# Moving convolution sums behind the softmax terms, and three weight spreadings to the end of their slices, in a fused attention and convolution kernel

## Chip, cores, metric

The kernel runs on one core of a Trainium2 chip. The metric is device microseconds of one execution, median of several runs. PE is TensorE, DVE is VectorE, ACT is ScalarE, POOL is GpSimd, SP is SyncE, which here issues nearly all DMAs.

## What is computed

The input x has 16 images of 56 x 56 pixels and 384 channels. Two layers follow each other, each with a residual and each behind a group normalisation over 32 groups:

```
x = x + attention(group_norm(x))      # layer 0
x = x + depthwise3x3(group_norm(x))   # layer 1, weights sign(clip(w))
```

Attention projects to q, k, v (384 to 1152), splits the channels into 3 groups of 4 heads of 32, and for each pixel takes a softmax over the 9 neighbours of a 3 x 3 window whose dilation is 1, 2 or 3 by group:

```
attn = softmax(einsum('bgdn,bgdkn->bgnk', q, unfold(k)) * 32**-0.5)
out  = einsum('bgnk,bgdkn->bgnd', attn, unfold(v))
y    = out @ w_proj.T + b_proj
```

All data is float32.

## The kernel before

An image is cut into 7 chunks of 8 rows (448 pixels); there are 112 chunks m, and c is the chunk's place in its image. Work is written as pieces that are put on a list of slices with `at(when, order, piece)`. Pieces are emitted by slice, and inside a slice by `order`, a number of the list at the end (SOFTMAX 0, SCORE 1, STATISTICS, CONVOLVE, WEIGH, QUERY, SPREAD, QKV, PROJECT, STAGE_A, STAGE_C, NORM, LOADS). A chunk advances every 9 slices (STEP), so several chunks are in flight. The tile framework's scheduler then makes each engine's instruction order out of what was emitted, and sets semaphores and buffers; it may move an instruction against its neighbours, except where `in_one_go` keeps matmuls together. Every engine runs its own order, SP too.

`plan_a` loads a chunk and transposes it (PE writes `pt_x`, ACT copies to `xa`, DVE takes statistics, SP stores it to `xd`).

`plan_b(m, t0)`, t0 = 9m, is the attention of one chunk:

- `k_or_v` and `query` (L463): PE projects into `pkv` and `pq`; ACT copies `pkv` to the k and v tiles (L473).
- `score(i)`, i = 0 to 8 (slice t0+i): DVE multiplies q with three shifted windows of k into `t` (L516). At i = 2, 5, 8 PE sums over the 32 channels of each head into `ps` (L501, 128x32 column tiles, 8, 8 and 11 matmuls).
- `softmax_1` to `softmax_5` (slices t0+9 to t0+12): ACT copies `ps` to `sT`, PE transposes it into `pt_s`, DVE and ACT make the softmax `ew`. Then `ew` is split into three bf16 terms that add up to it, all in the tile `e`: ACT casts the first (L555), POOL subtracts it (`rest`, L559), casts the second (L563) and subtracts for the third (L564).
- `turn_weights` (L569): SP issues one transposing DMA of `e` into `aT`.
- `weigh(i)`, i = 0 to 8 (slice t0+14+i): three bf16 matmuls spread `aT` over the channels into `pb_a` (L582, row tiles of 24 rows; one PSUM buffer of three banks). DVE multiplies with windows of v into `w` (L589). POOL adds the products (L597) and at every third i adds the three taps into `y` (L600, L601).
- `out_project(j)`: PE multiplies `y` with w_proj into `po` (L615); DVE adds bias and residual into `xr`, takes statistics, and SP stores to `x1d`.

`plan_c(m, t0)`, t0 = 9(m + 10), is the convolution of one chunk, ten chunks later. Channels 0 to 255 are convolved by PE (`convolve`: `pc`, L710, 32-column tiles). Channels 256 to 383 are done without PE: ACT scales nine shifted windows of `zg` into three `m` tiles (`taps_g`, L761), POOL adds these (L767), then the three planes and the residual (`sum_g`, L772, L775) into `xg`. `turn` transposes the result into `pt_o`, ACT copies it to `osb`, SP stores it. Where c = 0 the pieces `normalise_g` and `taps_g` come one slice later (`late`), for they need the statistics of the whole image. The last image (b = 15) takes another way, with DVE.

Seen from plan_c's chunk m, the softmax of chunk m + 9 falls into the slices t0 to t0+3.

Small PSUM results (`pt_x`, `pt_o`, `pt_s`, `pkv`, `po`, `pc`) rotate over three banks (`ps_mt`): each is written when the reader of the third before it has finished.

Of the kernel before, what the change touches and what calls it, by code (L numbers as in the profile page):

```python
# [1 line left out]

# [10 lines left out]
ALU = mybir.AluOpType  # L13
# [10 lines left out]
ROWS = 8  # L24
# [11 lines left out]
def dilated_attention_then_binary_conv(  # L36
# [28 lines left out]
    nc = tc.nc  # L65
# [10 lines left out]
    def place(p):  # L76

        g, o = divmod(p, NTAP)
        return NG * o + g
# [82 lines left out]
    for which, slots in enumerate((K_SLOTS, V_SLOTS)):  # L162
        kv.append([])
        for g, d in enumerate(DIL):
            kv[which].append([])
            for s in range(slots):
                t = const.tile([P, ROWS + 2 * d, W + 2 * d], F32, name=f"{'kv'[which]}_{g}_{s}")
# [11 lines left out]
    for s in range(2):  # L179
        t = const.tile([P, ROWS + 2, W + 2], F32, name=f"zg_{s}")  # L180
# [100 lines left out]
    def rows(ap):  # L281
        return ap.rearrange("p (r w) -> p r w", w=W)

    def three(t, d, ky):

        tw = t[:, ky * d : ky * d + ROWS, 0:W]
        return bass.AP(tw.tensor, tw.offset, [tw.ap[0], (d, 3), *tw.ap[1:]])

    def in_one_go(matmuls):

        matmuls[0]()
        with tc.high_priority():
            for m in matmuls[1:]:
                tc.keep_in_program_order(m())
# [97 lines left out]
    def at(when, order, piece):  # L392

        pieces.setdefault((when, order), []).append(piece)
# [2 lines left out]
    xd, x1d = {}, {}  # L397
    mr0, mr1 = {}, {}
    first = {}

    def plan_a(m, t0):

# [42 lines left out]
    def plan_b(m, t0):  # L445

        b, c = divmod(m, NCH)
        had = {}
# [102 lines left out]
        term = [e3.rearrange("p s u (r k) -> p (s u r) k", r=4)[:, :, 8 * t : 8 * t + 8] for t in range(TERMS)]  # L551
# [9 lines left out]
        def softmax_5():  # L561
            r8 = had["rest"].rearrange(EIGHTS, k=8)
            nc.gpsimd.tensor_copy(term[1], r8)  # L563
            nc.gpsimd.tensor_tensor(term[2], r8, term[1], ALU.subtract)  # L564

        def turn_weights():

# [5 lines left out]
        def weigh(i):  # L573

            g, ky = divmod(i, 3)
            pb = ps_bc.tile([P, 3, 512], F32, tag="bc", name="pb_a")

            def copy(kx):
                v = place(3 * i + kx)
                lo = 32 * (v // 2 % 4)  # L580
                rows_of = slice(lo, lo + 2 * TERMS * HEADS)
                return nc.tensor.matmul(  # L582
                    pb[:, kx, :PX].rearrange("p (s n) -> p s n", s=NSUB), spread[rows_of, v % 2, :],
                    had["a"][rows_of, :, v // 8, :], start=True, stop=True
                )

            in_one_go([lambda kx=kx: copy(kx) for kx in (2, 0, 1)])
            w = w_p.tile([P, 3, PX], F32, tag="w", name="w")
            nc.vector.tensor_tensor(  # L589
                w.rearrange("p k (r w) -> p k r w", w=W),  # L590
                pb[:, :, :PX].rearrange("p k (r w) -> p k r w", w=W), three(kv[1][g][m % V_SLOTS], DIL[g], ky), ALU.mult,
            )
            if ky == 0:
                had["w0"] = w
                return
            w0 = had["w0"]
            nc.gpsimd.tensor_tensor(w0, w0, w, ALU.add)  # L597
            if ky == 2:
                had[f"y{g}"] = y = y_p.tile([P, PX], F32, tag="y", name="y")
                nc.gpsimd.tensor_tensor(y, w0[:, 0], w0[:, 1], ALU.add)  # L600
                nc.gpsimd.tensor_tensor(y, y, w0[:, 2], ALU.add)  # L601
# [34 lines left out]
        at(t0 + 11, SOFTMAX, softmax_3)  # L636
        at(t0 + 11, SOFTMAX, softmax_4)
        at(t0 + 12, SOFTMAX, softmax_5)
        at(t0 + 12, LOADS, turn_weights)
        for i in range(9):  # L640
            at(t0 + 14 + i, WEIGH, lambda i=i: weigh(i))
        at(t0 + 20, LOADS, load_residual)
        for j in range(NG):
            at(t0 + 24 + j, PROJECT, lambda j=j: out_project(j))
# [1 line left out]
    def plan_c(m, t0):  # L646

        b, c = divmod(m, NCH)
        p0 = c * PX
        had = {}  # L650
# [93 lines left out]
        def taps_last(ky):  # L744
# [5 lines left out]
            for kx in range(3):  # L750
# [3 lines left out]
                    acc if o else mid, op0=ALU.mult, op1=ALU.add,  # L754
                )

        def taps_g(ky):
            t = m_p.tile([P, 3, PX], F32, tag="m", name="m")
            for kx in range(3):
                o = 3 * ky + kx  # L760
                nc.scalar.activation(  # L761
                    rows(t[:, kx]), zp[:, ky : ky + ROWS, kx : kx + W], AF.Copy, scale=ktap[:, o : o + 1]
                )
            if ky == 0:
                had["m"] = t
            else:
                nc.gpsimd.tensor_tensor(had["m"], had["m"], t, ALU.add)  # L767

        def sum_g(kx):
            t = had["m"]  # L770
            if kx < 3:
                nc.gpsimd.tensor_tensor(t[:, 0], t[:, 0], t[:, kx], ALU.add)  # L772
            else:
                mid = had["xg"][:, 1 : ROWS + 1, :].rearrange("p r w -> p (r w)")
                nc.gpsimd.tensor_tensor(mid, t[:, 0], mid, ALU.add)  # L775

        def turn(s):
            pt = ps_mt.tile([P, 512], F32, tag="mt", name="pt_o")
# [32 lines left out]
        for ky in range(3):  # L811
            at(t0 + 2 * ky + late, CONVOLVE, lambda ky=ky: taps_g(ky))
        for kx in (1, 2, 3):
            at(t0 + 5 + kx, CONVOLVE, lambda kx=kx: sum_g(kx))
# [5 lines left out]
        for s in range(NSUB):  # L820
            at(t0 + 9 + s, STAGE_C, lambda s=s: turn(s))

    SOFTMAX, SCORE, STATISTICS, CONVOLVE, WEIGH, QUERY, SPREAD, QKV, PROJECT, STAGE_A, STAGE_C, NORM, LOADS = range(13)

    STAT_ORDER = (STATISTICS, SPREAD, SPREAD, SPREAD, STATISTICS, SPREAD)
    STEP = 9
# [45 lines left out]
    for m in range(N):  # L872
        plan_a(m, start_a(m))
        plan_b(m, STEP * m)
        plan_c(m, STEP * (m + 10))
# [31 lines left out]
```

## Time and profile before

| what | us |
|---|---|
| median of 3 runs | 5328.02 (5322.63 to 5328.53) |
| profiled execution | 5318.41 |
| its span | 5316.7 |
| PE busy | 5131.6 (97%) |
| DVE busy | 4206.7 (79%) |
| POOL busy | 4255.0 (80%) |
| ACT busy | 2310.1 (43%) |
| mean granted TensorE clock | 0.981 |

The profile is one execution of the program. A line of the timeline gives the start, the duration, engine, source line, operation, what it writes and reads, and the shape; idle time before it and what ended it stand in brackets. Matmuls overlap, so what one of them costs is the distance from its start to the next start. An fp32 matmul of these leaves two records, so "x6" of `po` are three matmuls. A stage's row gives its length, each engine's busy time with its instructions, then the granted clock (1.00 is full), the share of the DMA engines, and GB/s. In the middle of the run a chunk takes about 44 to 46 us.

### The profile page before, as it was taken

The numbers are of one execution on the slowest core, as the hardware profiler recorded it, in microseconds if no ns is written. First come the engines' busy times: TensorE is split into PE (matmuls) and PEld (weight loads), VectorE is DVE, ScalarE is ACT, GpSimd is POOL, SyncE is SP. The second block draws the span as 40 slices with busy tenths as digits, with TensorE's granted clock in tenths as the row PEclk, the third lists the DMA queues.
The fourth block names the chain that finished last, engine by engine and source line by source line (L and its number), as shares of the span: only waits on it lengthen the run. The fifth ranks groups of instructions, "written<-read, shape, count | busy, mean of one in ns | idle before, by whom it ended". The sixth has DMA issues, their size and how long they took to land. (4 is left out here: it accounts for less than half of the span.)

```text
span 5316.7 us, 75544 instructions
## 1 busy us (share of the span) xinstructions
PE 5131.6 (97%) x26885; PEld 2336.1 (44%) x26885; DVE 4206.7 (79%) x4125; ACT 2310.1 (43%) x4077; POOL 4255.0 (80%) x2950
## 2 busy tenths in 40 slices
PE   8999999999999999999999999999999999999976
PEld 4444444444444444444444444444444444444433
DVE  5887887878878788887888878788887888878764
ACT  3223444444444444444444444444444444444443
POOL 2677888888888888888888888888888888888881
PEclk8999999999999999999999999999999999999987
DMA  6434565556555565666555556555565555554545
GB/s 194 134 105 116 165 164 158 164 156 163 162 158 161 157 164 157 165 161 165 161 159 164 150 161 165 162 161 160 166 165 155 162 149 164 146 137 134 134 133 155
DMA packets 811630, 825.62 MB, mean 155 GB/s; under 512 B 360307, under 2 KB 801014, under 8 KB 811254
## 3 DMA queue, kind: packets, MB, share of 16 engines
q1 hardware_dynamic: 803270, 808.79, 55.5%
q10 hardware_dynamic: 7984, 12.00, 0.7%
q8 instruction: 213, 3.49, 0.3%
q14 instruction: 163, 1.34, 0.1%
HBM read 466.41 MB, written 231.21 MB: 131 GB/s over the span
## 5 line engine op out<-in xcount | busy, mean ns | idle before, releaser
L597 POOL TENSOR_TENSOR w<-w 128x1344 f32<-128x1344 f32 x672 | 2071.5, 3083 | 522.1 <-DVE w L589 500.8
L589 DVE TENSOR_TENSOR w<-pb_a,v 128x1344 f32<-128x1344 f32 x1008 | 1555.3, 1543 | 274.0 <-PE pb_a L582 235.8
L516 DVE TENSOR_TENSOR t<-pq,k 128x1344 f32<-128x1344 f32 x1008 | 1536.8, 1551 | 251.5 <-PE pq L463 251.0
L463 PE MATMUL pkv<-xn,wqkvT 128*128 128x448 f32 x3924 | 1565.9, 548 | 0.4 <-DVE xr L618 0.4
L463 PEld LDWEIGHTS pkv<-xn,wqkvT 128*128 128x128 f32 x3924 | 718.4, 190 | 668.8 <-issue 643.0
L615 PE MATMUL po<-y,wprojT 128*128 128x448 f32 x2016 | 835.2, 551 | 41.8 <-POOL y L601 32.4
L696 ACT ACTIVATE z<-z,mrz 96x448 f32<-96x448 f32 x840 | 578.4, 751 | 662.9 <-DMA z<-x1d 427.6
L463 PE MATMUL pq<-xn,wqkvT 128*128 128x448 f32 x1962 | 856.0, 572 | 0.0
L767 POOL TENSOR_TENSOR m<-m 128x1344 f32<-128x1344 f32 x210 | 640.1, 3048 | 152.9 <-ACT m L761 148.8
L501 PE MATMUL ps<-t,sel 128*32 128x448 f32 x6048 | 659.4, 545 | 7.9 <-DVE t L516 6.9
L761 ACT ACTIVATE m<-zg,ktap 128x448 f32<-128x448 f32 x945 | 555.5, 659 | 8.6 <-POOL xg L775 1.7
L615 PEld LDWEIGHTS po<-y,wprojT 128*128 128x128 f32 x2016 | 376.9, 192 | 400.8 <-issue 336.2
L710 PE MATMUL pc<-z,kdiag 96*32 96x440 f32 (+1 forms) x5040 | 515.5, 542 | 4.8 <-POOL z L698 4.4
L463 PEld LDWEIGHTS pq<-xn,wqkvT 128*128 128x128 f32 x1962 | 352.0, 194 | 327.3 <-issue 327.3
L582 PE MATMUL pb_a<-aT,spread 24*128 24x448 bf16 x3024 | 369.6, 360 | 71.7 <-DMA aT<-e 60.4
L618 DVE SCALAR_TENSOR_TENSOR xr<-po,bias,xr 128x448 f32<-128x448 f32 x336 | 228.5, 680 | 220.0 <-PE po L615 215.1
L601 POOL TENSOR_TENSOR y<-y,w 128x448 f32<-128x448 f32 x336 | 381.6, 1136 | 16.3
L600 POOL TENSOR_TENSOR y<-w 128x448 f32<-128x448 f32 x336 | 381.4, 1135 | 13.6
L473 ACT COPY v<-pkv 128x448 f32<-128x448 f32 x336 | 176.3, 525 | 487.8 <-PE pkv L463 470.0
L717 DVE TENSOR_TENSOR x<-pc,x 128x448 f32<-128x448 f32 x224 | 138.5, 618 | 276.1 <-PE pc L710 275.9
L582 PEld LDWEIGHTS <-spread 24*128 24x128 bf16 x3024 | 98.5, 91 | 560.9 <-issue 481.0
L473 ACT COPY k<-pkv 128x448 f32<-128x448 f32 x336 | 178.8, 532 | 381.0 <-PE pkv L463 381.0
(132 smaller groups left out, 4311.0 us busy)
## 6 DMA issues: line engine op xcount, KB each, us to landing
z<-x1d SPq DMA_DIRECT2D x570, 224.0 KB, 3.9
xr<-xd SPq DMA_DIRECT2D x112, 672.0 KB, 4.2
x1d<-xr SPq DMA_DIRECT2D x112, 672.0 KB, 3.2
xn<-xd SPq DMA_DIRECT2D x109, 672.0 KB, 4.6
xin<-in_x_dram SPq DMA_DIRECT2D x105, 672.0 KB, 7.2
xd<-xa SPq DMA_DIRECT2D x315, 224.0 KB, 3.4
out_dram<-osb SPq DMA_DIRECT2D x420, 168.0 KB, 3.5
x<-x1d SPq DMA_DIRECT2D x112, 448.0 KB, 8.2
```

The costliest lines, as they stand in the source:

```text
L463: nc.tensor.matmul(dst[:, :PX], wqkvT[:, cc, o0 : o0 + P], had["xn"][:, cc, :], start=(cc == 0), stop=(cc == NG - 1))
L501: return nc.tensor.matmul(had["ps"][32 * j : 32 * j + 32, :PX], sel[:, s0 : s0 + 32], tk, start=(issued[j] == 1), stop=(issued[j] == len(r ...
L516: nc.vector.tensor_tensor(t.rearrange("p k (r w) -> p k r w", w=W), q3, k3, ALU.mult)
L582: return nc.tensor.matmul(pb[:, kx, :PX].rearrange("p (s n) -> p s n", s=NSUB), spread[rows_of, v % 2, :], had["a"][rows_of, :, v // 8, :] ...
L589: nc.vector.tensor_tensor(w.rearrange("p k (r w) -> p k r w", w=W), pb[:, :, :PX].rearrange("p k (r w) -> p k r w", w=W), three(kv[1][g][m ...
L597: nc.gpsimd.tensor_tensor(w0, w0, w, ALU.add)
L601: nc.gpsimd.tensor_tensor(y, y, w0[:, 2], ALU.add)
L615: nc.tensor.matmul(po[:, :PX], wprojT[:, g, j * P : (j + 1) * P], had[f"y{g}"], start=(g == 0), stop=(g == NG - 1))
L696: nc.scalar.activation(z, z, AF.Identity, bias=mrz[:, j, q, 0:1], scale=mrz[:, j, q, 1:2])
L710: return nc.tensor.matmul(pcr[q * HD : (q + 1) * HD, :, lo:hi], kdiag[:, kx, j * NQ + q, :], rows(set_of(j, q))[:, :, lo + kx - 1 : hi + k ...
L761: nc.scalar.activation(rows(t[:, kx]), zp[:, ky : ky + ROWS, kx : kx + W], AF.Copy, scale=ktap[:, o : o + 1])
L767: nc.gpsimd.tensor_tensor(had["m"], had["m"], t, ALU.add)
```

## The change

Two things are changed.

The POOL sums of the convolution get an order of their own where c = 0: the last sum of taps (ky = 2) and the three pieces of `sum_g` are told to be issued on POOL behind the last softmax term of chunk m + 9. `tc.issue_after(ins)` adds, to each instruction of its block, an edge for the order on the engine, with no semaphore.

The pieces `weigh(2)`, `weigh(5)` and `weigh(8)` of each chunk get a later place inside their slice, WEIGH_LATE, behind CONVOLVE, PROJECT, STAGE_A and STAGE_C. The next slice begins with the score of i = 8, 2 or 5 of the next chunk, whose `ps` matmuls then follow.

```diff
+    last_term = {}
...
         def softmax_5():
             r8 = had["rest"].rearrange(EIGHTS, k=8)
             nc.gpsimd.tensor_copy(term[1], r8)
-            nc.gpsimd.tensor_tensor(term[2], r8, term[1], ALU.subtract)
+            last_term[m] = nc.gpsimd.tensor_tensor(term[2], r8, term[1], ALU.subtract)
...
         for i in range(9):
-            at(t0 + 14 + i, WEIGH, lambda i=i: weigh(i))
+            at(t0 + 14 + i, WEIGH_LATE if i % 3 == 2 else WEIGH, lambda i=i: weigh(i))
...
+        def behind_softmax(wanted):
+            if c or not wanted:
+                return nullcontext()
+            return tc.issue_after(last_term[m + 9].ins)
+
         def taps_g(ky):
...
             if ky == 0:
                 had["m"] = t
             else:
-                nc.gpsimd.tensor_tensor(had["m"], had["m"], t, ALU.add)
+                with behind_softmax(ky == 2):
+                    nc.gpsimd.tensor_tensor(had["m"], had["m"], t, ALU.add)
 
         def sum_g(kx):
             t = had["m"]
-            if kx < 3:
-                nc.gpsimd.tensor_tensor(t[:, 0], t[:, 0], t[:, kx], ALU.add)
-            else:
-                mid = had["xg"][:, 1 : ROWS + 1, :].rearrange("p r w -> p (r w)")
-                nc.gpsimd.tensor_tensor(mid, t[:, 0], mid, ALU.add)
+            with behind_softmax(True):
+                if kx < 3:
+                    nc.gpsimd.tensor_tensor(t[:, 0], t[:, 0], t[:, kx], ALU.add)
+                else:
+                    mid = had["xg"][:, 1 : ROWS + 1, :].rearrange("p r w -> p (r w)")
+                    nc.gpsimd.tensor_tensor(mid, t[:, 0], mid, ALU.add)
...
-    SOFTMAX, SCORE, STATISTICS, CONVOLVE, WEIGH, QUERY, SPREAD, QKV, PROJECT, STAGE_A, STAGE_C, NORM, LOADS = range(13)
+    SOFTMAX, SCORE, STATISTICS, CONVOLVE, WEIGH, QUERY, SPREAD, QKV, PROJECT, STAGE_A, STAGE_C, WEIGH_LATE, NORM, LOADS = range(14)
```

On PE this changes, in a chunk in the middle of the run (groups of matmuls in their order):

```
before  pb_a pkv pt_x pt_o pb_a pt_o ps pc pb_a pq pt_x pt_o pb_a pkv pt_o pb_a pt_x ps pc pb_a pq pb_a pkv po pb_a po ps pb_a pq po pt_s
after   pb_a pkv pt_x pt_o pt_o pb_a ps pc pb_a pq pt_x pt_o pb_a pkv pt_o pt_x pb_a ps pc pb_a pq pb_a pkv po po pb_a ps pb_a pq po pt_s
```

More of the change, by code (lines that the diff above doesn't have):

```diff
@@ L1 @@
-from contextlib import ExitStack
+from contextlib import ExitStack, nullcontext
 import concourse.bass as bass
```

## The prediction

> **What bounds the kernel now.** I read the page first: the span and the busy shares.
>
> ```profile
> span 5316.7 us, 75544 instructions
> PE 5131.6 (97%) x26885; PEld 2336.1 (44%) x26885; DVE 4206.7 (79%) x4125; ACT 2310.1 (43%) x4077; POOL 4255.0 (80%) x2950
> ```
>
> PE is the bound; VectorE and GpSimd are a fifth idle. So only two things can shorten the run: fewer PE nanoseconds per chunk, or fewer PE waits. For the second, the list of waits (engine line waited for: total us, times, longest):
>
> ```profile
> PEld L582 <- DMA aT<-e: 78.3, 23, 4.8
> ...
> PE pb_a L582 <- DMA aT<-e: 60.4, 20, 4.0
> ```
>
> The spreading matmuls `pb_a` wait for the transposed weights `aT`, 60.4 us in 20 waits. Laid along the timeline, twelve waits of 4.0 us lie one per image (320 us apart), always in the slices of plan_c's first chunk (c = 0). One of them, POOL's timeline (start, duration):
>
> ```profile
> 2398.04 3.03 POOL L767 TENSOR_TENSOR m<-m 128x1344 f32<-128x1344 f32 x1
> 2401.15 1.39 POOL L772 TENSOR_TENSOR m<-m 128x448 f32<-128x448 f32 x1
> 2402.50 3.06 POOL L597 TENSOR_TENSOR w<-w 128x1344 f32<-128x1344 f32 x1
> 2405.54 1.12 POOL L772 TENSOR_TENSOR m<-m 128x448 f32<-128x448 f32 x1
> ...
> 2407.72 1.15 POOL L559 TENSOR_TENSOR rest<-ew,e 112x512 f32<-112x512 f32 x1
> ...
> 2410.48 1.14 POOL L775 TENSOR_TENSOR xg<-m,xg 128x448 f32<-128x448 f32 x1
> 2411.59 1.15 POOL L564 TENSOR_TENSOR e<-rest,e 112x512 bf16<-112x512 f32 x1
> ```
>
> Four sums of the convolution (3.03 + 1.39 + 1.12 + 1.14 us) stand ahead of the last softmax term. It ends at 2412.74, SP issues the transpose at 2412.77, and PE, and the stages' granted clock, show:
>
> ```profile
> 2411.19 1.71 PE L501 MATMUL ps<-t,sel 128*32 128x448 f32 x16
> 2416.81 0.36 PE L582 MATMUL pb_a<-aT,spread 24*128 24x448 bf16 x3 [3.91 <-DMA aT<-e]
> 2417.11 4.22 PE L463 MATMUL pq<-xn,wqkvT 128*128 128x448 f32 x6
> 2412.80:2416.80 4.00, 0.10 (x4) 0.00 (x0) 0.12 (x1) 0.00 (x0) 3.92 (x2) 1.00 0.73 134
> 2416.80:2421.30 4.50, 4.49 (x13) 1.94 (x17) 1.56 (x1) 0.00 (x0) 4.27 (x3) 0.62 1.08 291
> ```
>
> The wait is 4.0 us, and behind it the clock is 0.62: `pq` takes 4.14 us to the next start instead of 2.46. Then an undisturbed stage:
>
> ```profile
> 2517.42 2.42 PE L615 MATMUL po<-y,wprojT 128*128 128x448 f32 x6
> 2519.77 0.37 PE L582 MATMUL pb_a<-aT,spread 24*128 24x448 bf16 x3
> 2520.12 2.52 PE L615 MATMUL po<-y,wprojT 128*128 128x448 f32 x6
> 2522.57 2.46 PE L501 MATMUL ps<-t,sel 128*32 128x448 f32 x22
> ...
> 2527.61 2.42 PE L615 MATMUL po<-y,wprojT 128*128 128x448 f32 x6
> 2529.87 0.60 PE L536 MATMUL pt_s<-perm,sT 128*112 128x128 f32 x4
> ```
>
> Here starts are to be subtracted. A `po` group with 128x128 groups on both sides takes 2.26 us (2527.61 to 2529.87); with `pb_a` behind it 2.35; with `pb_a` ahead and `ps` behind 2.45. So passing from 128x128 to the row-tiled `pb_a` or the column-tiled `ps` costs about 0.10 us, and coming back from `pb_a` another 0.10. `pb_a` takes 0.29 (0.35 here). Where `pb_a` stands directly before `ps` (a dozen places in the start-up) both keep their usual times.
>
> [...] 4.0 us idle, then 1.4 to 2.4 us lost in that stretch, varying by image.
>
> **The change, part by part.** It adds and removes no arithmetic; it moves instructions, in each engine's order as follows.
>
> (1) *Sums behind the terms* (c = 0, images 0 to 14). POOL now runs w, w, rest, y, e, y, e, then the four sums. Worked for the image shown: the second `w` needs VectorE's product, which ended at 2399.5, and runs 2399.55 to 2402.6; ACT's first term is there at 2402.2; rest 2403.75, y 2404.9, e 2405.5, y 2406.6, last term 2407.7, five us earlier. The DMA took 4.0 us from issue to PE's start, so `aT` is there at about 2411.8. SP is free from 2403.5; two issues (xd, out) that stood ahead of the transpose now stand behind it, harmless. PE wants `aT` at 2412.5, and in the new order a `pq` matmul of 0.95 us stands ahead, so 2413.5: **slack 1.7 us, the wait goes**, and with it the slow clock. In twelve images that is 48.1 us of wait plus 22.4 us of slow clock (sum of the excess of pq's time in each) = 70.5. Images 0, 13 and 14 show smaller ones, 8.5 us together; I take 6. The split `pq` costs a mode change both ways, 0.2 x 15 = 3. Net 73.5.
> What is late next: the sums end at 2414.2 instead of 2411.6, the next two `w` at 2420.3, `y` at 2422.5 (was 2421.2), while PE is 6 us earlier. The next `po` reads that `y` in its third matmul, at 2424.3: slack 1.8. VectorE's next product needs the buffer freed at 2417.2 and comes at 2418.7. The sums' reader, `pt_o`, comes a chunk later. All covered, none by much.
>
> (2) *WEIGH_LATE*: three sites per chunk.
> Site A (`pt_o pb_a pt_o ps`, now `pt_o pt_o pb_a ps`): starts in the timeline give 425 + 295 + 470 ns up to `ps`. Now a pt_o without mode change (425 - 98 = 327), one with `pb_a` behind it (425) and pb_a (294), 1046 against 1190: 144 ns less. But the second pt_o needs the PSUM bank that ACT's copy of k frees 0.80 us after pkv, and would now start at 0.385 + 0.327 = 0.71: 80 ns are lost again. 63 ns x 86 chunks = 5.4.
> Site B (`pt_o pb_a pt_x ps`, now `pt_o pt_x pb_a ps`): 423 + 296 + 533 against 327 + 480 + 294: 151 ns x 79 = 11.9. VectorE's statistics of pt_x now stand ahead of the product `w`, which starts 1.4 us later; behind it in VectorE's queue is `x`, which needs the next `pc`, and the next pb_a is 3.9 us away, so both are covered. POOL's sum of that product follows 1.4 us later; it idles 1.1 us before it and 1.2 after it.
> Site C (`po pb_a po ps`, now `po po pb_a ps`, shown above): 199 ns less. But the second `po` needs the bank that ACT's copy of v frees. That copy waits behind z, zg and six taps, a chain that starts at the last softmax term (SP issues nine DMAs after the transpose). In the chunk shown v ended at 2520.06 and po started at 2520.12. Over 87 chunks v ends -1.5 to 3.7 us after the first po's start. Before, po was not ready until 2.65; now it is at 2.25, and sites A and B bring it another 0.21 nearer to the chain. With these 87 values the mean of the site is -0.04 us: x 94 = -3.9. VectorE's product (behind xr, stats and xr) must now end within 2.68 us of pb_a's start, or the next pb_a waits; it ends at about 2.4. POOL's sum of it stays where it was, behind the taps' sums.
> Sum of (2): 13.4. Bounds: no copy in the way 43; chain another 0.5 us later, about -15.
>
> (3) Start-up, chunks 4 to 9: `pb_a` waits 1.8 us for `aT` after the second `ps`; a `pq` matmul now stands between: 0.95 - 0.2, six times, 4 us. The tail after the last weights is rearranged; no row of before shows the new order; nearest are its own waits of 9.8 and 1.8 us, which stay, so I take 0, with 3 us to both sides.
>
> Sum: 73.5 + 13.4 + 4 = **91 us**. The profiled execution took 5318.4 (span 5316.7), so 5227; the median of the runs is 9.6 above that execution: **5237**.
>
> **Rivals.**
> *Copies are no obstacle* (the chain to v follows PE and the earlier z loads): 43 instead of 13, and 8.5 in place of 6: -123, 5205. For it: in more than half of the chunks v is early. Against: the k copy at site A is exact to 10 ns.
> *The wait is only halved*: SP, POOL or a busier DMA delays `aT` by 3 to 4 us more than worked, or the backlog of sums makes `po` wait. About -35 to -50 in all, 5280. For it: slacks below 2 us. Against: in other chunks the same POOL order meets PE with 2.8 us to spare.
> *The change doesn't do what it says*: the terms are early already where PE doesn't wait, so nothing changes but the sites and the start-up, at most 17 us (5311), or nothing where the copies take that (5328). Against it: POOL's timeline above.
> *Slower*: ACT's in-order queue at site C. Every us by which v's copy comes later than now is a us of PE wait in some 80 chunks. It decides from a mean of about 1.1 us later (91/80); at 1.6 us the kernel is at 5365. For it: the chain hangs on SP's queue behind the transpose. Against: the last term moves by only 0.06 us against PE outside c = 0.
>
> **How the numbers follow.** Worked case 0.54, copies no obstacle 0.17, halved wait 0.19, nothing changes 0.04, slower 0.06. The range reaches from the second case to the third, with a few us of spread between runs: 5198 to 5290. A measurement of this kernel can tell about 0.2% (11 us) from no change; faster 0.91, same 0.03, slower 0.06.
>
> **What would show it.** Right: the waits for `aT` fall from 60 us to under 10, the clock after c = 0 stays at 1.00, POOL shows the four sums behind the last term; PE shows `pb_a` directly before `ps`; at site C waits of PE for ACT's v copy grow from about 10 us to some 25. Wrong: 4 us holes at c = 0 remain, or `po` waits for `y` after them, or v ends over 3 us after the first po in most chunks.

## The result, and the profile after

| | us | ratio to before |
|---|---|---|
| before, median of 4 runs | 5325.42 (5322.63 to 5328.53) | |
| after, median of 4 runs | 5280.55 (5279.62 to 5283.21) | 0.9916 [0.9899, 0.9934] |
| profiled execution after | 5280.6, span 5278.8 | |

The ratio is to the kernel before, with its 95% interval. The change gains 45 us. The forecast was 5237, a gain of 88 against this median of before: the direction was right, the size was half. The page of the kernel after, span and busy times:

```profile
span 5278.8 us, 75494 instructions
...
PE 5099.7 (97%) x26885; PEld 2333.3 (44%) x26885; DVE 4208.9 (80%) x4125; ACT 2298.1 (44%) x4077; POOL 4254.9 (81%) x2950
```

PE is busy 32 us less with the same instructions; ACT is 12 us less busy, VectorE and POOL are as they were. The waits of the kernel after (engine line waited for: total us, times, longest; PEld is PE's loading of weights):

```profile
PEld po L616 <- ACT v L474: 80.8, 76, 2.7
...
PE pb_a L583 <- DVE w L590: 39.2, 21, 7.2
PE po L616 <- ACT v L474: 38.8, 41, 1.9
...
PE pb_a L583 <- DMA aT<-e: 4.1, 5, 1.1
```

The wait for `aT` fell from 60.4 to 4.1 us, as forecast. In its place stand two waits (PE's `po` for ACT's copy of v, `pb_a` for VectorE's product `w`) that were short before:

```profile
PE pb_a L582 <- DVE w L589: 11.3, 7, 2.0
...
PE po L615 <- ACT v L473: 9.4, 16, 1.0
```

So 56 us of waits went and 57 came. What is left as a gain lies mostly in PE's busy time, which fits less slow clock (mean granted clock 0.981 before, 0.985 after) and fewer mode changes, by which is meant here a passing of PE between the 128x128 groups and the row- or column-tiled ones (about 0.10 us each by the starts in the trace before).

**The first chunk of an image**, first POOL's timeline of the kernel after (start, duration):

```profile
2389.33 1.17 POOL L560 TENSOR_TENSOR rest<-ew,e 112x512 f32<-112x512 f32 x1
...
2393.23 1.15 POOL L565 TENSOR_TENSOR e<-rest,e 112x512 bf16<-112x512 f32 x1
2394.35 3.03 POOL L777 TENSOR_TENSOR m<-m 128x1344 f32<-128x1344 f32 x1
...
2400.99 6.19 POOL L598 TENSOR_TENSOR w<-w 128x1344 f32<-128x1344 f32 x2
```

The sums (L777 and the ones behind it) now follow the last term, and the products' sums follow them without a gap. PE's timeline there, then the row of that stage (length, busy times of PE, PEld, DVE, ACT, POOL, then the clock, DMA share, GB/s):

```profile
2397.49 1.71 PE L502 MATMUL ps<-t,sel 128*32 128x448 f32 x16
2399.13 1.02 PE L464 MATMUL pq<-xn,wqkvT 128*128 128x448 f32 x2
2400.11 0.37 PE L583 MATMUL pb_a<-aT,spread 24*128 24x448 bf16 x3
...
2399.10:2402.10 3.00, 3.00 (x13) 1.10 (x9) 2.47 (x2) 0.00 (x0) 2.92 (x3) 1.00 0.79 225
```

`pb_a` comes at 2400.11 behind one `pq` matmul with no wait, and the clock is 1.00. It is a near thing: the transpose of this image was issued at 2394.41, and the view of `aT` in this stretch says how long it took to land:

```profile
DMA to landing us min/median/max: 5.6/5.6/5.6
```

A little later in the same chunk:

```profile
2409.38 2.42 PE L616 MATMUL po<-y,wprojT 128*128 128x448 f32 x6
2413.24 2.52 PE L616 MATMUL po<-y,wprojT 128*128 128x448 f32 x6 [1.44 <-ACT v L474]
```

Here is one of the new waits: the second `po` needs the bank that ACT's copy of v frees.

**Where the time went.** Site C of the prediction is slice 2, site A slice 5 and site B slice 8. Each chunk has one `pt_s`, so its starts on PE cut every run into the same 112 stretches. The stretch of chunk m goes from its `pt_s` to the next. The table gives their lengths in us, summed by place: up to the first of chunk 3, the start-up and the first image, then the chunks 14 to 104 by m mod 7 (13 stretches each). Stretch 1 holds an image's statistics and stretch 2 plan_c's c = 0. The columns on the right are experiments told below.

| chunks | before | after | sums alone | places alone | slice 5 kept | v on VectorE | sums, v on VectorE |
|---|---|---|---|---|---|---|---|
| up to `pt_s` of 3 | 213.2 | 216.6 | 212.8 | 216.2 | 212.8 | 218.4 | 213.4 |
| 3 to 8 | 248.6 | 243.5 | 248.7 | 243.5 | 243.4 | 243.4 | 247.1 |
| 9 | 52.5 | 53.1 | 55.0 | 49.1 | 53.1 | 53.1 | 55.4 |
| 10 to 13 | 177.8 | 177.9 | 177.8 | 178.2 | 176.3 | 176.3 | 177.8 |
| m mod 7 = 0 | 585.2 | 589.4 | 587.2 | 588.2 | 588.1 | 576.7 | 579.8 |
| 1 (statistics) | 611.5 | 634.0 | 611.5 | 633.9 | 614.1 | 623.4 | 613.9 |
| 2 (c = 0) | 658.0 | 595.9 | 589.6 | 655.5 | 591.8 | 581.5 | 584.2 |
| 3 to 6 together | 2310.0 | 2311.3 | 2312.6 | 2306.9 | 2305.6 | 2290.3 | 2307.6 |
| 105 to 111 and the end | 460.0 | 457.3 | 455.3 | 462.1 | 455.5 | 453.9 | 459.2 |
| span | 5316.7 | 5278.8 | 5250.6 | 5333.6 | 5240.7 | 5217.1 | 5238.4 |

The change gains 62 us at c = 0 and 5 in the start-up, loses 22.5 in the statistics stretch, 4 beside it and 3 at the very start, and brings nothing in the 52 ordinary stretches (3 to 6), where the new places were to save mode changes. Each column is one profiled execution, and the runs of one kernel differ by 3 to 17 us, so a difference of a few us in one row tells nothing.

### The profile page after: what moved, and what is told of

It reads as the page before. It is cut to its first block, busy times and chain, and to the rows that moved or that the text cites. A ratio compares the mean times of both kernels' runs of the same rounds, so it can differ in the third digit from the quotient of the medians.

```text
span 5278.8 us, 75494 instructions
## 1 busy us (share of the span) xinstructions
PE 5099.7 (97%) x26885; PEld 2333.3 (44%) x26885; DVE 4208.9 (80%) x4125; ACT 2298.1 (44%) x4077; POOL 4254.9 (81%) x2950
## 5 line engine op out<-in xcount | busy, mean ns | idle before, releaser
L616 PE MATMUL po<-y,wprojT 128*128 128x448 f32 x2016 | 824.2, 549 | 63.8 <-ACT v L474 38.8
L464 PE MATMUL pq<-xn,wqkvT 128*128 128x448 f32 x1962 | 839.8, 560 | 0.0
L777 POOL TENSOR_TENSOR m<-m 128x1344 f32<-128x1344 f32 x210 | 640.2, 3049 | 119.8 <-ACT m L770 115.5
L583 PE MATMUL pb_a<-aT,spread 24*128 24x448 bf16 x3024 | 369.1, 359 | 43.5 <-DVE w L590 39.2
L435 ACT COPY xa<-pt_x 128x448 f32<-128x448 f32 x315 | 168.5, 538 | 353.1 <-PE pt_x L423 352.9
```

The lines of the kernel that those rows point to most:

```text
L464: nc.tensor.matmul(dst[:, :PX], wqkvT[:, cc, o0 : o0 + P], had["xn"][:, cc, :], start=(cc == 0), stop=(cc == NG - 1))
L583: return nc.tensor.matmul(pb[:, kx, :PX].rearrange("p (s n) -> p s n", s=NSUB), spread[rows_of, v % 2, :], had["a"][rows_of, :, v // 8, :] ...
L616: nc.tensor.matmul(po[:, :PX], wprojT[:, g, j * P : (j + 1) * P], had[f"y{g}"], start=(g == 0), stop=(g == NG - 1))
```

## Experiments

Theory: the sums behind the terms do all that was forecast, and the new places lose by two waits, one for v at site C and one for the product of slice 5 in the statistics chunk. Rival: the sums bring less than was forecast, and the places gain. Before measured 5320.0, 5323.4 and 5319.0 beside the three sets of runs.

### The two parts apart

Sums alone:

```diff
-            at(t0 + 14 + i, WEIGH_LATE if i % 3 == 2 else WEIGH, lambda i=i: weigh(i))
+            at(t0 + 14 + i, WEIGH_LATE if False else WEIGH, lambda i=i: weigh(i))
```

> Part 1 alone: the convolution sums behind the last softmax term where c = 0; all nine spreadings stay in WEIGH. Theory (the change is a gain by part 1, partly eaten by part 2): the twelve 4.0 us waits for aT and the slow clock behind them go (-79 us), and at c = 0 the second po waits 0.4 to 1.5 us for ACT's copy of v, some 8 us in all: 5257 us, faster than the whole change by 20 or more. Rival (the sums' backlog on POOL hands the wait on, and part 2 is what brings the 45 us): 5300 or more, with waits of PE for POOL's y or VectorE's w after c = 0.

Places alone:

```diff
-            if c or not wanted:
+            if True or c or not wanted:
                 return nullcontext()
```

> Part 2 alone: weigh(2), (5), (8) late, sums where they were. Theory: mode changes save 43 us by the starts of before; the k copy takes back 7, ACT's v copy at site C about 42, the wait of pb_a for VectorE's product in the statistics chunk 22, the start-up gives 4: about 5349 us, slower than before by 0.4%. Rival (site C costs no more than the prediction had it, the 45 us are missing elsewhere, at c = 0): 5325 - 17 = 5308 or below.

Measured: sums alone 5251.88 us, ratio 0.9872 [0.9858, 0.9887]; places alone 5335.24, ratio 1.0023 [1.0014, 1.0033]. By the medians the first part alone is 29 us faster than the whole change, by the ratios 23; the second is a loss by itself. The theory holds in sign, and the rival falls on both; the loss of the places alone is about half of what the theory had (12 us by the ratio, against 24). In the table, sums alone wins 68.3 us in the c = 0 stretches and changes stretches 0, 1 and 3 to 6 by 2.7 us or less. Places alone keeps the hole at c = 0: the stretches take 655.5 us against 658.0, with waits for `aT` that are shorter (some 2.5 us instead of 4.0 in the twelve images) and 24.7 us of waits of `po` for v beside them. It has the loss in the statistics stretch in full (633.9).

### v's copy off ACT

```diff
-            nc.scalar.copy(cur[:, d : d + ROWS, d : d + W], rows(pk[:, :PX]))
+            if which and g == 2:
+                nc.vector.tensor_copy(cur[:, d : d + ROWS, d : d + W], rows(pk[:, :PX]))
+            else:
+                nc.scalar.copy(cur[:, d : d + ROWS, d : d + W], rows(pk[:, :PX]))
```

> The whole change, and the copy of v of group 2 (the one that frees the bank of site C's second po) moved from ACT to VectorE, so that it no longer stands behind z, zg and six taps in ACT's queue. Theory (that queue is what site C waits for): PE's wait for the copy of v falls from about 67 us to under 10, VectorE carries 112 more copies of 0.5 us beside PE: about 5230 us. Rival (the second po is late for another reason, or VectorE's extra copy delays the score products and ps waits instead): within 10 us of the whole change, 5270 to 5290.

Measured: 5222.37 us, ratio 0.9814 [0.98, 0.9829], on the theory's side, 8 us below its figure. The waits of `po` for v are gone from its list. PE's timeline at site C of that kernel:

```profile
2473.94 4.67 PE L619 MATMUL po<-y,wprojT 128*128 128x448 f32 x12
2478.55 0.36 PE L586 MATMUL pb_a<-aT,spread 24*128 24x448 bf16 x3
2478.84 2.46 PE L505 MATMUL ps<-t,sel 128*32 128x448 f32 x22
```

Both `po` groups run through in 4.61 us up to `pb_a`, and `pb_a` takes 0.29. An undisturbed ordinary stretch is 44.08 us, against 44.44 before: 0.36 us less per chunk is what the three places are worth. In the kernel after, 29 of the 52 ordinary stretches have 44.1 us or less and the others up to 47.94; here 51 of 52 do.

To see whether v's move is itself the gain, the same copy with all weights in their old places (the edit above and the one of the sums alone):

> The sums behind the terms and v's copy on VectorE, but all weights in their old place (the second part of the change taken out). It tells what the second part is worth once ACT's copy of v is out of its way. Theory (the mode changes saved are worth what they measure, 144 x 86 + 151 x 79 + 199 x 94 ns = 43 us, less 7 us for k's copy and 8 us for the statistics chunk, so 28): 5222.4 + 28 = 5250, which is the time of the kernel with the sums alone, so that v's move by itself brings nothing. Rival (v's move brings its own gain by relieving ACT, and the second part brings next to nothing even then): 5225 or less.

Measured: 5240.29 us, ratio 0.984 [0.9824, 0.9857]; neither 5250 nor 5225. So there is a square of four:

| median us | v on ACT | v on VectorE |
|---|---|---|
| weights in their old places | 5251.9 | 5240.3 |
| three weights last | 5280.6 | 5222.4 |

With v's copy on ACT the new places cost 29 us; with it on VectorE they bring 18. The four medians come from three sets of runs, in which the kernel before took 5325, 5320 and 5323 us; by the ratios to it the places cost some 23 and bring some 14. The sign is the same. (The two intervals in the right column overlap by a hair; the ordinary stretches, 44.38 against 44.04 us on average, speak for a real difference.) v's move by itself brings 12 (17 by the ratios), more than the theory's nothing; the old order had waits for v too, 17.4 us of PE in the list of the kernel with the sums alone.

### Which site makes v late

The later place at slices 5 and 8 only, so that site C is as before:

```diff
+            at(t0 + 14 + i, WEIGH_LATE if i in (5, 8) else WEIGH, lambda i=i: weigh(i))
```

> The whole change with the later place taken at two of the three sites only (slices 5 and 8); at slice 2, between the two po groups, the weights stay where they were. Theory (at site C the mode change saved, 0.199 us x 94 = 19, is less than the new waits for ACT's copy of v): against the changed kernel's 5280.6 the waits of PE's po for ACT's v fall by some 35 us and the 19 us come back, so 5264, with the waits for v near the 45 us that the kernel with the sums alone has. The product that waits in the chunk with the statistics (about 22 us in 13 images) stays. Rival (the waits for v have another cause, the first-chunk queue on SP, and site C only shows them): they stay, the 19 us are lost on top, and the kernel takes about 5298.

Measured: 5306.32 us, ratio 0.997 [0.9959, 0.9981]. Worse than both values. The trace shows an effect of the edit in the start-up, which has no site C: the stretches of chunks 3 to 9 take 322.4 us together, against 296.6 in the kernel after. PE's timeline of that kernel there:

```profile
286.27 0.36 PE L583 MATMUL pb_a<-aT,spread 24*128 24x448 bf16 x3 [3.22 <-DMA aT<-e]
```

With slice 2 back in place PE reaches the first weights of the next chunk over 3 us ahead of `aT` in five start-up chunks (3.2 to 3.4 us), and the clock behind each of these waits is 0.60 to 0.67. So the time of this run says nothing on site C. It was taken again with slice 2 late in the start-up:

```diff
+            at(t0 + 14 + i, WEIGH_LATE if (i in (5, 8) or (i == 2 and m < 10)) else WEIGH, lambda i=i: weigh(i))
```

> As the kernel with the later place at slices 5 and 8 only, but in the start-up chunks (m under 10) slice 2 takes the later place too, as in the changed kernel; so only site C of the full chunks is put back. The former edit lost 26 us in the start-up (chunk 3 to 10 of it took 322.4 us against 296.6), which had nothing to do with site C. Theory (in the full chunks ACT's chain to v's copy, and not the order at site C, sets the period; what sites A and B save is waited away there too): 5306.3 - 26 = 5280, the same as the changed kernel, and the chunks of the phases 3 to 6 keep their 44.4 us. Rival (site C taken alone is a loss of 19 us, the account with which the former edit was expected at 5264): 5262, the chunks of these phases at 44.2 us. Second rival (site C alone is a gain of its full mode change): 5299.

Measured: 5279.44 us, ratio 0.9925 [0.9908, 0.9942], the time of the whole change. Undisturbed stretches are now 44.28 us: sites A and B save 0.16, site C 0.20. Yet the 52 ordinary stretches take 2306.7 us against 2311.3, and stretch 0 585.9 against 589.4 (in the fastest of the four runs, 11 us below their median). PE's waits for v are 18.9 us here and 38.8 in the kernel after: the 19.9 us more are about what 94 savings of 0.20 us come to. So site C neither wins nor loses: what it saves, PE waits away there for v.

### The statistics chunk

```diff
+            at(t0 + 14 + i, WEIGH_LATE if i % 3 == 2 and not (i == 5 and m % NCH == 0) else WEIGH, lambda i=i: weigh(i))
```

> The whole change, except that weigh(5) stays in WEIGH in the one chunk per image whose slice also holds the mean of the statistics (m a multiple of 7). Theory: there VectorE's order is pair, ew, w, and ew, which ran 3.2 us beside a POOL sum, held w and so the next pb_a, 1.5 us in 13 images; with w ahead of ew that wait goes: about 5260 us. Rival (ew is only stretched because PE is ahead, the wait moves to the next product): within 5 us of the whole change.

Measured: 5243.35 us, ratio 0.9853 [0.9836, 0.9869]: 37 us better than the whole change by an edit in 16 chunks, where about 20 had been expected. POOL's, VectorE's and PE's timeline of the kernel after in a statistics stretch, then VectorE's in this one:

```profile
2652.93 3.04 POOL L598 TENSOR_TENSOR w<-w 128x1344 f32<-128x1344 f32 x1
...
2653.27 3.17 DVE L548 TENSOR_TENSOR ew<-ew,sm 112x432 f32<-112x432 f32 x1
2656.36 1.54 DVE L590 TENSOR_TENSOR w<-pb_a,v 128x1344 f32<-128x1344 f32 x1
...
2657.96 0.37 PE L583 MATMUL pb_a<-aT,spread 24*128 24x448 bf16 x3 [1.44 <-DVE w L590]
```

```profile
2634.24 1.51 DVE L590 TENSOR_TENSOR w<-pb_a,v 128x1344 f32<-128x1344 f32 x1
2635.65 1.89 DVE L548 TENSOR_TENSOR ew<-ew,sm 112x432 f32<-112x432 f32 x1
```

With slice 5 last, `pb_a` comes behind the six small `pm` matmuls, and VectorE takes the softmax's `ew` ahead of the product `w`. That `ew` takes 3.17 us where the product is delayed and 1.89 where it is not, and the next `pb_a` waits for the product. It is so in 12 of 13 images (3.15 to 3.20 us), and with slice 5 kept PE's waits of `pb_a` for `w` fall from 39.2 to 21.9 us. Of the 38 us of span, 19.8 lie in stretch 1. 3.8 lie at the start, by slice 5 of chunk 0; with it last, PE's timeline of the kernel after has a wait there of another kind, for POOL's arithmetic on the statistics, which is gone here:

```profile
181.46 1.43 PE L363 MATMUL pp<-pair,gselT 32*128 32x2 f32 x6 [3.77 <-POOL pair L357]
```

5.7 us in stretches 3 to 6 and 4.1 in stretch 2 were not expected; PE's waits for v are 9.4 us less in this run (29.4 against 38.8), and why was not followed up.

### The two stores behind the transpose

At c = 0 the xd and out stores now stand on SP between the transpose and the z loads. ACT took two of them:

```diff
+                queue = nc.scalar if j == 1 and t0 // STEP >= 17 and (t0 // STEP - 10) % NCH == 0 else nc.sync
+                queue.dma_start(xd[b][j * P : (j + 1) * P, c * PX : (c + 1) * PX], xa)
...
-            queue = nc.sync if b < B - 1 else nc.scalar
+            queue = nc.sync if b < B - 1 and not (c == NCH - 1 and s == 2) else nc.scalar
```

> The whole change with two stores per image, the store of a term of x (j = 1 of the chunk that is being prepared) and the last store of an output chunk, issued by ACT's queue instead of SP's, so that behind the transpose of the first chunk SP comes to the z loads at once. Theory (these two issues, which the change moved behind the transpose, hold the z loads and with them ACT's copy of v back by about 2 us in the first chunk of 12 images): v ends up to 1.3 us earlier against the first po there, about 0.8 us less wait in each of 12 images, so 8 to 10 us less than the changed kernel's 5280.6: 5271. [...] Rival (the stores are harmless, as the prediction had it, and the chain to v is late for its length): 5280, and the waits for v at the first chunk stay at 2.6 us behind the start of po.

Measured: 5277.77 us, ratio 0.9914 [0.99, 0.9929], not to be told from the whole change: the forecast of 5271 fails. SP's timeline in the same image (SPq is SP issuing a DMA), first of the kernel after, then with the stores on ACT:

```profile
2394.41 1.55 SPq L570 DMA_TRANSPOSE aT<-e  x1
2396.05 1.20 SPq L438 DMA_DIRECT2D xd<-xa  x1
2397.35 0.39 SPq L801 DMA_DIRECT2D out_dram<-osb  x1
2397.83 1.35 SPq L685 DMA_DIRECT2D z<-x1d  x2
```

```profile
2398.91 1.54 SPq L571 DMA_TRANSPOSE aT<-e  x1
2400.55 1.17 SPq L479 DMA_DIRECT2D k<-k  x1
2401.81 1.01 SPq L686 DMA_DIRECT2D z<-x1d  x2
```

The first issue behind the transpose takes 1.20 us in the one, a store, and 1.17 in the other, a halo copy of k, which took the place of the stores, so z starts 2.9 us behind the transpose instead of 3.4; before it was 1.65, with z directly behind. At c = 0, on average of 13 images, v's copy ends 2.61 us behind the start of the first `po`; it was 3.05 in the kernel after and 0.47 before. The edit thus brought z forward by 0.5 us of the 1.8 that the change had cost it, and v by 0.44. That SP's order there is part of the delay is seen, that it is all of it is not shown: the run does not test a z that starts directly behind the transpose.

### Both mends together

v on VectorE, and slice 5 kept in place in the statistics chunk.

> The whole change, with the copy of v on VectorE instead of ACT, and with slice 5 left in place in the chunk that has the statistics (13 times). Theory (of the 22 us that PE waits in the statistics chunk, 8 us are left once v is off ACT, since VectorE's order there is another): 5222.4 - 8 = 5214. Rival (the two costs are independent and add): 5222.4 - 37 = 5185, with 37 the difference between the changed kernel and the one with slice 5 left in place.

Measured: 5221.83 us, ratio 0.9812 [0.9797, 0.9826], the same as with v on VectorE alone. It misses 5214 by more than the spread of its runs, and 5185 by far. The start, up to chunk 3, falls from 218.4 to 213.6 us, but the statistics stretches take 626.0 us instead of 623.4. PE's timeline of this kernel in that stretch:

```profile
3265.17 0.35 PE L339 MATMUL pv<-dev,gsel 128*32 128x2 f32 x6 [1.52 <-POOL dev L333]
```

POOL is busy without a gap of 0.1 us for the 24 us ahead of this, with the convolution's sums at their start: here PE waits for POOL's backlog. Such waits of `pv` come to 5.6 us in 7 places, and with v on VectorE alone they were there already, 5.2 us in 6. Why the two mends do not add is seen in the trace with v on VectorE alone: PE's waits of `pb_a` for `w` in the 13 statistics stretches are 2.6 us there, against 17.3 in the kernel after, so the second mend had little left to mend. The rest of what the statistics stretch keeps was not followed up. This version and the one with v on VectorE alone are the fastest, 1.9% below the kernel before.

## Why the prediction was half right

- **Part 1, sums behind the terms: right.** Forecast 73.5 us; alone it brings 68 by the medians of its set (5320.0 to 5251.9), 68.3 in the c = 0 stretches. The clock stays at 1.00 in the image shown, and behind c = 0 in images 1 to 12 PE waits for no later `w` or `y`, as worked. The worked slack of 1.7 us is there in nine of these twelve images (1.64 to 1.72 us). In the other three, the image shown among them, the transpose took 5.6 to 5.8 us from issue to landing instead of 4.0, and PE came just as the tile landed. So the wait went in all twelve, but in three with nothing to spare, which was luck: the prediction took 4.0 us for all, where the trace before has transposes of up to 5.4. The first image pays instead of gaining a little: its stretch 9 is 2.5 us longer (4.0 on top of the places), with one 7.2 us wait of `pb_a` for `w` there in the kernel after, and VectorE idle for 8.7 us ahead of it, for ACT's copy `xa`. In the trace before PE waited in that image for `w` (1.3 us), `t` (1.6) and `y` (2.1), not for `aT`, so there was no hole for the sums to close. That they would displace work there was not priced.
- **Part 3, start-up: right.** Forecast 4; the stretches 3 to 8 fell by 5.1 us.
- **Part 2, the sites: wrong, and in sign.** Forecast 13.4 gained; on top of part 1 the places cost 29 by the medians and 23 by the ratios (start-up included), more than the prediction's own lower bound of -15. Three steps failed.
  - *Site A, "63 ns x 86 chunks"*. The saving is there (sites A and B together 0.16 us, worked 0.21), but only the chunks of the ordinary order were counted. In the 13 with `pm` the move turns VectorE's order of `ew` and `w`: their stretch is 22.5 us longer, and 19.8 us come back when slice 5 is kept there. At the start the same slice brings the wait of 3.8 us for `pair`. This term was missing, and it is the largest.
  - *Site C, "mean -0.04"*. The saving of the mode change is right (0.20 us). The loss was taken from v's times in the trace before, shifted by 0.21 us. The waits of PE for v rose from 9.4 to 38.8 us instead of 25. In the ordinary stretches the places were to give some 0.14 us a chunk (13.4 over 94), 7 us in 52; they gave 3.0 by themselves and 1.3 on top of the sums. The waits for v grew by about what was saved, which a shift of fixed times does not show; that v's copy is itself tied to PE's pace, through what stands ahead of it in ACT's queue, is a reading and was not traced.
  - *"Two issues (xd, out) ... harmless"*, and what is late next at c = 0. With the 4 us hole gone PE comes to site C earlier, and v, which had ended 0.47 us after the first `po` began, ends 3.05 after (2.80 with the sums alone, where `po` is ready only at 2.65). With the places that costs 6.3 us in the c = 0 stretches (595.9 against 589.6).
- **The rivals.** "The wait is only halved" has the measured number, 5280, but not its mechanism: the waits for `aT` went. Of its causes a slower DMA was seen, but by 1.6 to 1.8 us in three images, not by the 3 to 4 us that it asked for. The stated range reached as far as 5290 only for the sake of this rival, so that the measured time lies in it is luck. "Copies are no obstacle" is what v on VectorE comes near to: 5222, against 5205 worked. "Slower through ACT's queue at site C" had the right place. It needed 1.1 us of delay on average to decide; in the ordinary stretches it came to 0.37 us a chunk (44.45 on average against 44.08), enough to eat the saving and no more.

## What to carry over

Test a reordering on every form of the order, not only on the commonest: a chunk with six additional small matmuls had another order on a second engine and cost more than the sites brought once the waits for v are taken off. A saving at a point that waits for a copy in another engine's queue may be waited away there (site C saved 0.20 us in each of 94 chunks, and PE's waits for v grew by 19.9 us), so ask first whether the queue would follow; moving that one copy to another engine turned a loss of 23 to 29 us into a gain of 14 to 18. When a long wait goes, list what it had covered, and look at the queue order behind it instruction by instruction. And work a slack out with the slowest DMA of its kind in the trace, not with a usual one.

## What had not been expected of the hardware

- **`ew` on VectorE beside a sum on POOL.** The same 112x432 multiplication takes 0.58 to 0.61 us where POOL runs nothing when it starts (68 of 112 times in the kernel after), and 3.17 us when it starts 0.34 us after POOL's 128x1344 sum `w`. Of the 44 that start while a POOL instruction runs, 43 end 0.46 to 0.47 us after that instruction does, whatever was left of it; in the kernel before it is so in all 47. With `w` first, `ew` starts later in a POOL sum and takes 1.89. The product `w`, which reads `pb_a` and v, is not stretched so: all 1008 of them in the kernel after take 1.49 to 1.57 us, 827 of them started while a POOL instruction ran. Why the one is held and the other not is not shown.
- **The issue behind a DMA transpose.** On SP it takes 1.20 us (median) instead of the usual 0.4 to 0.6, for stores, halo copies and loads of z alike (medians 1.17 to 1.24), in the kernels before and after. In the run with two stores on ACT, moving them away from there only brought up the next.
- **How long a wait slows the clock.** A stretch at a lower granted clock followed all twelve waits of 3.9 to 4.0 us at c = 0 before (0.50 to 0.66 in the 4.5 us behind each), and all five of 3.2 to 3.4 us in the start-up of the kernel with slice 2 in place (0.60 to 0.67). Of the seven waits of 1.7 to 1.9 us for `aT` in the kernel before, it followed two (1.71 and 1.75 us; clock 0.64 and 0.62) and not the other five (1.70 to 1.89 us; 1.00). What sets these apart is not shown.
